# Weight blocks of the first FFN stage read from the weights themselves, and the sums of weights spread over other places

## The chip, the cores and the metric

The kernel runs on one core of a Trainium2 chip. The metric is the device time of one execution in microseconds; lower is better. Times given for a kernel are a median of several executions, and one further execution is profiled.

Engine names follow the profile: PE is TensorE (matrix products), DVE is VectorE, ACT is ScalarE, POOL is GpSimd, SP is SyncE, which issues transfers and does no arithmetic. Transfers issued by SP go through one DMA queue (q1 in the profile), those issued by POOL through another (q0). [...]

## The reference

The input x is 2 x 2048 rows of 1024 numbers, in float32. A pre-norm attention layer with one head of 256 is followed by a pre-norm feed-forward layer (FFN), cut here to what is computed:

```python
x = x + attn(layernorm(x))            # qkv = x @ Wqkv + bqkv; softmax(q k^T / 16) v; @ Wo + bo
h = layernorm(x)
logits = h @ gate_w                   # 8 experts; the two largest logits are added
r = relu(h @ up_w) ** 2               # up_w 1024 x 2048
shared = r @ down_w                   # down_w 2048 x 1024
latent = (h @ fc1_w) @ expert_w       # fc1_w 1024 x 512, expert_w 512 x 512
routed = (latent * top2_sum) @ fc2_w  # fc2_w 512 x 1024
x = x + layernorm(shared + routed) * ln_gamma + ln_beta
```

## The kernel before

**Arithmetic.** Every float32 factor is split into a rounded part and the rest, and a product is three matmuls: high x high, low x high, high x low (class `Pass3`). A "cast" on ACT makes the high part, a subtraction on DVE the low one.

**Stages.** The rows form 8 blocks of 512 (`NBLK`). First `begin` folds expert_w into fc2_w (kept in DRAM as `fc2e`) and prepares the first block; then q, k and v are made block by block (`a_block`, `qkv_block`), then attention runs over the blocks. In attention's loop `n` counts from 1 to 8: the scores of block n are made beside the value products of block n - 1, then `finish(n - 1)` and `project(n - 1)` apply Wo. `project` loads four residual rows on SP, adds bo to them by four accumulating transfers on POOL (L638, the last one kept in `last[0]`), and stores the finished rows on SP. Attention is ordered by a scheduler; `begin`, the q/k/v blocks before the last, and the FFN are in the order written.

**FFN as a seven-product scheme.** The FFN takes two blocks of rows at a time (`b` = 0 to 3) and has two stages: s = 0 multiplies by up_w and fc1_w side by side, s = 1 by down_w and fc2e one above the other. Each stage treats its weight as 2 x 2 quarters and does seven block products p1 to p7 (Strassen's scheme in Winograd's form). Three of them take a quarter of the weight as it is: p1 takes (0,0), p2 takes (1,0), p3 takes (1,1). Four take sums of quarters, numbered 1 to 4 (`RIGHT`, L777). Each product's weight comes in NK = 10 pieces of 128 x 512, so a stage has 70 pieces of 12 or more matmuls; `m` counts the pieces of the first stage.

**Sums of weights.** `sum_tile(s, q)` are DRAM tiles (`wt`), of 2 MB and 0.5 MB for each s and q. `sum_step(i)` (L387) copies one quarter into such a tile with two POOL transfers (L391); this serves for sums' first terms and also for the three plain quarters of each s. For some i it also adds the second term of an earlier sum with two accumulating transfers (L399). There are 14 steps: three in the q/k/v blocks i = 4, 5, 6 (L703) and 11 in attention, at k = 2 and k = 8 of the loops n = 2 to 7 (L746), each placed after the last bo addition issued.

**Pieces.** `stage` (L797) takes a tile `w` (pools `wk` with six and `wv` with one) and loads a piece on SP into its second half; `cast_piece` writes the high part into the first half on ACT; `end_piece` subtracts on DVE and, for pieces that are used again by a later b, stores the pair with one 512 KB POOL transfer (`w_p`, L844). Later uses load the pair and need no split. `next_piece` keeps up to three pieces ready, one cast and two loading. `wk`, `wv`, `spp` and `gp` lie in memory that attention's pools `ex` for keys and values gave back: `wk` in that of the keys, the others in that of the values. `spp` (four tiles) holds split left factors in the second stage and nothing in the first.

**Order around the start of the FFN.** The first pieces of b = 0 are loaded, cast and subtracted while attention still runs: the scheduler places them among the last scores. In b = 0 of the first stage, p1's first four pieces come first, then p1 and p2 alternate (`up_order(4)`), until m = 19; p4 follows at m = 20 to 29, p6 at 30 to 39, p5 at 40 to 49, p3 at 50 to 59 and p7 at 60 to 69. Beside them the object `norm2` normalises the second block's rows: each `step` (L942) loads a row on SP, takes moments on ACT, normalises, transposes on DVE, and writes and fetches the transposed row on POOL, in different steps for different rows, 11 steps in all. At L1156 they are spread over m = 0 to 13; from m = 12 on (`m4`, L1161) the fetched tiles are split for p4.

Of the kernel before, what the change touches and what calls it, by code (L numbers as in the profile page):

```python
# [9 lines left out]
FP = mybir.dt.float32  # L10
FR = mybir.dt.float32r
AF = mybir.ActivationFunctionType
ALU = mybir.AluOpType
# [4 lines left out]
P = 128  # L18
SQ = 32
W = 512  # L20
# [5 lines left out]
def kernel(  # L26
# [69 lines left out]
    def f32(t):  # L96
        return t.bitcast(FP)
# [223 lines left out]
    def transpose_tile(r, t, xT):  # L321

        for g in range(NCC // 4):
            pt = bank(psc, "pt")
            for j in range(4):
                nc.tensor.transpose(pt[:, ts(j, P)], r[:, ts(4 * g + j, P)], ident)
            hi, lo = (v.rearrange("p (c n) -> p c n", n=W)[:, :, ts(t, P)] for v in xT[g])
            split(pt.rearrange("p (c n) -> p c n", n=P), hi, lo)
# [30 lines left out]
    def as_piece(t, s):  # L359

        return t.rearrange("p (c n) -> p c n", n=P) if s == 0 else t

    def quarter(s, a, b):

        if s == 0:
            return [w[ts(a, HC), ts(b, n)] for w, n in ((up_w, HU), (fc1_w, HL))]
        return [w[ts(a, n), ts(b, HC)] for w, n in ((down_w, HU), (fc2e, HL))]

    def sum_tile(s, q):

        if (s, q) not in tsum:
            shapes = [(HC, n) if s == 0 else (n, HC) for n in (HU, HL)]
            tsum[s, q] = [
                dram.tile(list(sh), FP, name="wt_{}_{}_{}".format(len(tsum), s, i))
                for i, sh in enumerate(shapes)
            ]
        return tsum[s, q]

    FIRST = {1: (0, 1), 2: (1, 1), 3: (0, 1), 4: (1, 0)}
    SUMS = [(s, q) for s in range(2) for q in (1, 3, 2, 4)]
    COPIES = SUMS + [(s, q) for s in range(2) for q in ((0, 0), (1, 0), (1, 1))]
    ADDS = dict(zip((4, 5, 6, 8, 9, 10, 11, 13), SUMS))
    last = [None]

    def sum_step(i):  # L387

        s, q = COPIES[i]
        for o, t in zip(sum_tile(s, q), quarter(s, *FIRST.get(q, q))):  # L390
            nc.gpsimd.dma_start(out=o, in_=t)  # L391
        if i in ADDS:
            s, q = ADDS[i]
            if q % 2:
                terms = quarter(s, *((0, 0) if q == 1 else (1, 1)))
            else:
                terms = sum_tile(s, q // 2)
            for o, t in zip(sum_tile(s, q), terms):
                nc.gpsimd.dma_start(out=o, in_=t, accum_op=ALU.add, max_dma_last_dim=4096)  # L399


    kv = {}
# [55 lines left out]
    def begin(wqkv, xT):  # L458

        ew, f2_0 = (unit(a, FP) for a in ("ew", "f2_0"))  # L460
        ev = ew.rearrange("p (c n) -> p c n", n=LAT)
        for i in range(NLC):
            nc.sync.dma_start(out=ev[:, :, ts(i, P)], in_=cols(expert_w, i, P))
        for i in range(NLC):
            nc.sync.dma_start(out=f2_0[:, ts(i, W)], in_=fc2_w[ts(i, P), 0:W])
        f2 = [f2_0]
        first = load_block(xf, order[0])
        f2.append(load("f2_1", cols(fc2_w, 1, W))[1])

        ws = {i: load(f"w{i}", cols(Wqkv, i, D)) for i in (2, 0)}  # L470
        rows = load_block(xf, order[1])
        ws[1] = load("w1", cols(Wqkv, 1, D))
        nc.gpsimd.dma_start(out=bqk_sb, in_=bqkv[0 : 2 * D].rearrange("(f p) -> p f", p=P))
        nc.gpsimd.dma_start(out=bv_sb, in_=bqkv[2 * D : 3 * D].partition_broadcast(P))

        eh, el = unit("eh"), unit("el")
        for mc in range(NLC):
            pt = bank(psc, "pt")
            for lc in range(NLC):
                nc.tensor.transpose(pt[:, ts(lc, P)], ew[:, ds(lc * LAT + mc * P, P)], ident)  # L480
            split(pt, eh[:, ts(mc, LAT)], el[:, ts(mc, LAT)])

        def split_f2(h, eng):
            f2h, f2l = unit(f"f2h{h}"), unit(f"f2l{h}")
            for mc in range(NLC):
                split(f2[h][:, ts(mc, W)], f2h[:, ts(mc, W)], f2l[:, ts(mc, W)], eng)
            return f2h, f2l

        def fold(f2hl, first=None):
            accs = [Pass3(bank(psa, "pf"), NLC) for _ in range(NLC)]  # L490
            for mc in range(NLC):
                if first:
                    first(mc)
                for lc in range(NLC):
                    accs[lc].add(
                        piece((eh, el), mc, LAT, ts(lc, P)), piece(f2hl, mc, W, slice(0, W))
                    )
            return accs

        def folded(h, accs):  # L500
            r = unit(f"fold{h}", FP)
            for lc in range(NLC):
                nc.scalar.copy(r[:, ts(lc, W)], accs[lc].ps)
            return r

        accs = fold(split_f2(0, nc.vector))
        stats = [row_stats(first[0])]
        for t in range(NB):
            if t + 1 < NB:
                stats.append(row_stats(first[t + 1]))  # L510
            normalise(first[t], stats[t])
            if t == 0:
                f2hl = split_f2(1, nc.gpsimd)
            elif t == 2:
                wqkv[2] = split_unit(*ws[2], nc.gpsimd)
        r = [folded(0, accs)]
        r.append(folded(1, fold(f2hl, lambda t: transpose_tile(first[t], t, xT))))
        wqkv[0] = split_unit(*ws[0])
        wqkv[1] = split_unit(*ws[1], nc.gpsimd)
        return NormBlock(rows), r  # L520
# [169 lines left out]

    wqkv, xT = {}, new_xT("a")
    with tc.manual_schedule():
        norm, fold = begin(wqkv, xT)
        x3 = lambda: None
        steps = list(range(len(COPIES)))
        for i in range(NBLK - 1):
            norm, xT, x3 = a_block(i, norm, xT, x3)
            if i == 0:
                for h in range(C // W):
                    nc.gpsimd.dma_start(  # L700
                        out=cols(fc2e, h, W), in_=fold[h].rearrange("p (c n) -> p c n", n=W)
                    )
            if i >= NBLK // 2:  # L703
                sum_step(steps.pop(0))
    a_block(NBLK - 1, None, xT, x3)

    wo_f = [load_row(Wo[ts(dc, P), :]) for dc in range(NDC)]
# [75 lines left out]
            order += ([("p1", i + lag)] if i + lag < NK else []) + [("p2", i)]  # L783
        return order + [(p, i) for p in ("p4", "p6", "p5", "p3", "p7") for i in range(NK)]

    UPS = [up_order(4 if b == 0 else 1) for b in range(NBLK // 2)]
    DOWN = [(p, i) for p in ("p1", "p2", "p6", "p5", "p3", "p7", "p4") for i in range(NK)]
    NBB = NBLK // 2
    pieces = [(b, s, *w) for b in range(NBB) for s in range(2) for w in (UPS[b], DOWN)[s]]
    kept, staged, cast, ready = {}, [], [], []  # L790
    LATE = 5

    def source(s, q, i):
        t, j = (tsum[s, q][0], i) if i < HU // P else (tsum[s, q][1], i - HU // P)
        return t[:, ts(j, P)].rearrange("(c p) i -> p c i", p=P) if s == 0 else t[ts(j, P), :]

    def stage():  # L797


        b, s, p, i = pieces.pop(0)  # L800
        if len(pieces) < LATE and early:
            staged.append((early.pop(0), False, None))
            return
        n_w[0] += 1
        w = (wk if n_w[0] % 7 else wv).tile([P, 2 * W], FR, tag="w", name="w")
        if (s, p, i) in kept:
            nc.sync.dma_start(out=w.bitcast(FP), in_=kept[s, p, i])
            staged.append((w, False, None))
            return
        nc.sync.dma_start(out=as_piece(f32(w)[:, W : 2 * W], s), in_=source(s, RIGHT[p], i))  # L810

        if s == 1 and p in ("p3", "p7", "p4"):
            keep = b == 2 and p == "p4" and i >= NK - LATE
        else:
            keep = b == 1 or i % 2 == 0
        staged.append((w, True, (s, p, i) if keep else None))

    early, n_w = [], [0]  # L820

# [7 lines left out]
    def cast_piece():  # L829

        w, raw, key = staged.pop(0)
        if raw:
            nc.scalar.copy(w[:, 0:W], f32(w)[:, W : 2 * W])  # L833
        cast.append((w, raw, key))

    def end_piece():

        w, raw, key = cast.pop(0)
        if raw:
            v = f32(w)  # L840
            nc.vector.tensor_tensor(w[:, W : 2 * W], v[:, W : 2 * W], v[:, 0:W], ALU.subtract)  # L841
        if key:
            kept[key] = dram.tile([P, 2 * W], FP, name="w_{}_{}_{}".format(*key))
            nc.gpsimd.dma_start(out=kept[key], in_=w.bitcast(FP))  # L844
        ready.append((w[:, 0:W], w[:, W : 2 * W]))
# [187 lines left out]
    with tc.manual_schedule():  # L1033
        for b in range(NBB):
# [72 lines left out]
            for m, (p, i) in enumerate(UPS[b]):  # L1107
# [45 lines left out]

                if m % 2 and m < 17:
                    out_step()
                if b == 0 and m in (0, 1, 2, 4, 6, 8, 9, 10, 11, 12, 13):  # L1156
                    norm2.step()
                if b == 0 and m < NB:
                    split_x(x_t[0], 1, m, X["p2"], split_late)

                m4 = 12 if b == 0 else 10  # L1161
                if m == m4:
                    x_t[1] = norm2.x
                    X["p4"] = new_x()
# [172 lines left out]
```

## Time and profile before

| what | value |
|---|---|
| median of 3 runs (lowest to highest) | 2360.73 us (2359.38 to 2362.85) |
| the profiled execution's own time | 2357.94 us |
| its span, first to last instruction | 2355.8 us |
| PE busy / DVE / ACT / POOL | 2323.3 / 1501.8 / 1168.1 / 285.4 us |
| mean granted PE clock | 0.997 |
| moved by DMA, mean rate | 572.54 MB, 243 GB/s |
| w<-wt: piece loads from sums and copies (SP) | 280 of 256 KB |
| w_p<-w: pieces kept (POOL) | 115 of 512 KB |
| wt<-up_w and wt<-down_w (POOL), copies and additions | 9 + 9 of 2 MB |
| wt<-fc1_w and wt<-fc2e (POOL) | 9 + 9 of 0.5 MB |
| wt<-wt: second terms that are sums themselves (POOL) | 4 of 2 MB, 4 of 0.5 MB |

How to read it: the span is a little shorter than the execution's time, because work around the program's instructions is not in it. Where one engine is busy for nearly all of the span, time is found in the few stretches in which it waits, and the wait's releaser tells which transfer or engine ended it. In the lists of waits, a line gives who waited for whom, the total in us, how often, and the longest. In a timeline, the columns are start, duration, engine, line, operation, output and inputs, and in brackets the idle time before it and what ended that.

The stages in the profiled execution: q/k/v to about 310 us, attention to about 775 us with the FFN's first products mixed in from 752 us, then four rounds of the FFN.

### The profile page before, as it was taken

How to read it: one execution, taken by the hardware profiler on the slowest of the kernel's cores; microseconds unless marked ns; L12 is line 12 of the kernel's file. 1: busy time of each engine (PE TensorE's matmuls, PEld its weight loads, DVE VectorE, ACT ScalarE, POOL GpSimd, SP SyncE). 2: the span in 40 equal slices, each digit the busy share in tenths (PEclk: the TensorE clock that was granted, in tenths of full speed). 3: DMA queues.
4: the chain of work that ended last, by engine and by line, in shares of the span. 5: the costliest groups of instructions: out<-in, count | busy, mean ns of one | idle time of the engine just before them, and what ended most of it. 6: DMA issues, size and time to landing. Idle time of an engine off the chain costs nothing.

```text
span 2355.8 us, 29360 instructions
## 1 busy us (share of the span) xinstructions
PE 2323.3 (99%) x10704; PEld 1919.4 (81%) x10704; DVE 1501.8 (64%) x2238; ACT 1168.1 (50%) x1916; POOL 285.4 (12%) x425
## 2 busy tenths in 40 slices
PE   8999999999999999999999999999999999999997
PEld 7888888888887778788788888878888877888886
DVE  5566559888877575797645577753456683435656
ACT  6555455555544643667552374743055564214245
POOL 3232111011110110111110011110000021000001
PEclk9999999999999999999999999999999999999999
DMA  5977884999997766786897789786567589665674
GB/s 197 318 256 276 286 205 127 296 315 323 286 253 211 250 208 191 228 276 209 265 316 242 229 297 319 229 267 227 193 204 278 194 267 331 189 191 187 204 247 134
DMA packets 222208, 572.54 MB, mean 243 GB/s; under 512 B 18368, under 2 KB 80320, under 8 KB 220016
## 3 DMA queue, kind: packets, MB, share of 16 engines
q1 hardware_dynamic: 152160, 315.67, 39.9%
q0 software_dynamic: 69904, 255.00, 36.1%
q8 instruction: 85, 1.39, 0.2%
q14 instruction: 59, 0.48, 0.1%
HBM read 430.61 MB, written 197.66 MB: 267 GB/s over the span
## 4 chain that ended last, share of the span: by engine, by line
PE 91%; DMA 3%; issue 3%; DVE 1%; ACT 1%; POOL 0%; SPq 0%; POOLq 0%; DVEq 0%; ACTq 0%
PE pu L130 31%; PE pd L130 28%; PE po L130 7%; PE pq L130 7%; PE ps L130 7%; PE pv L130 4%; PE pw L130 4%; DMA w<-wt 2%; PE pg L890 1%; PE pf L130 1%; PE psum L622 1%; DMA xt<-xt_d 0%; DVE w L841 0%; DMA ew<-in_L_ffn_expert_w_dram 0%; DMA res<-x 0%
## 5 line engine op out<-in xcount | busy, mean ns | idle before, releaser
L130 PE MATMUL pd<-w,sp 128*128 128x512 f32 x3336 | 759.0, 389 | 4.9 <-DVE y L1274 4.8
L130 PEld LDWEIGHTS pd<-w,sp 128*128 128x128 f32 x3336 | 625.5, 188 | 137.3 <-ACT nm L260 6.0
L130 PE MATMUL pu<-xh,w 128*128 128x512 f32 x2240 | 692.8, 390 | 0.1
L130 PEld LDWEIGHTS pu<-xh,w 128*128 128x128 f32 x2240 | 419.2, 188 | 89.9 <-DVE w L841 1.5
L130 PE MATMUL pu<-xl,w 128*128 128x512 f32 x1120 | 436.2, 389 | 0.9 <-DVE xl L150 0.9
L841 DVE TENSOR_TENSOR w<-w 128x512 fp32r<-128x512 f32 x280 | 191.6, 687 | 99.0 <-ACT w L833 92.0
L833 ACT CAST w<-w 128x512 fp32r<-128x512 f32 x280 | 170.9, 615 | 166.2 <-DMA w<-wt 155.6
L130 PEld LDWEIGHTS pu<-xl,w 128*128 128x128 f32 x1120 | 210.2, 188 | 45.1 <-DVE xl L150 1.4
L1077 ACT CAST sp<-h 128x512 fp32r<-128x512 f32 x238 | 146.3, 618 | 151.9 <-PE pd L130 125.6
L1082 DVE TENSOR_TENSOR sp<-h,sp 128x512 fp32r<-128x512 f32 x238 | 162.9, 687 | 68.1 <-ACT sp L1077 67.9
L130 PE MATMUL po<-p,v 128*128 128x512 f32 x768 | 194.3, 391 | 0.6 <-DVE p L143 0.6
L130 PE MATMUL ps<-q,k 128*128 128x512 f32 x768 | 192.5, 390 | 1.5 <-DVE max L565 1.5
L130 PEld LDWEIGHTS ps<-q,k 128*128 128x128 f32 x768 | 143.6, 188 | 31.8 <-DVE max L565 1.9
L130 PEld LDWEIGHTS po<-p,v 128*128 128x128 f32 x768 | 143.0, 188 | 30.2 <-DVE p L143 1.0
L150 DVE TENSOR_TENSOR xl<-xt,xh 128x512 fp32r<-128x512 f32 x108 | 74.4, 689 | 134.9 <-ACT xh L149 134.9
L1027 ACT ACTIVATE h<-h 128x1024 f32<-128x1024 f32 x48 | 50.7, 1055 | 208.8 <-DVE h L1137 159.8
L560 ACT COPY s<-ps 128x512 f32<-128x512 f32 x128 | 75.0, 587 | 133.5 <-PE ps L130 133.4
L213 DVE STREAM_TRANSPOSE xblk<-xrow 128x1024 f32<-128x1024 f32 x60 | 121.1, 2018 | 9.6 <-ACT xrow L283 9.6
L844 POOL DMA_DIRECT2D w_p<-w x115 | 61.6, 536 | 508.7 <-DVE w L841 435.0
L565 DVE TENSOR_TENSOR max<-ps,max 128x512 f32<-128x512 f32 x120 | 82.4, 687 | 36.3 <-ACT s L560 36.1
L130 PE MATMUL pq<-xha,w_h 128*128 128x512 f32 x256 | 99.7, 389 | 0.0
L130 PE MATMUL pq<-xha,w_l 128*128 128x512 f32 x256 | 99.7, 389 | 0.0
(181 smaller groups left out, 3031.8 us busy)
## 6 DMA issues: line engine op xcount, KB each, us to landing
w<-w_p SPq DMA_DIRECT2D x280, 512.0 KB, 4.2
w<-wt SPq DMA_DIRECT2D x280, 256.0 KB, 3.4
w_p<-w POOLq DMA_DIRECT2D x115, 512.0 KB, 4.6
xt_d<-xblk POOLq DMA_DIRECT2D x56, 512.0 KB, 4.4
xt<-xt_d POOLq DMA_DIRECT2D x56, 512.0 KB, 6.7
wt<-in_L_ffn_up_w_dram POOLq DMA_DIRECT2D x9, 2048.0 KB, 23.8
wt<-in_L_ffn_down_w_dram POOLq DMA_DIRECT2D x9, 2048.0 KB, 31.1
xres<-in_L_attn_x_dram SPq DMA_DIRECT2D x32, 512.0 KB, 11.2
```

What stands on the lines that cost most here:

```text
L130: nc.tensor.matmul(self.ps, lhsT=a, rhs=b, start=self.i == 0, stop=self.i == self.n - 1, skip_group_check=self.on,)
L150: late_ops.append(lambda: nc.vector.tensor_tensor(lo, t, f32(hi), ALU.subtract))
L213: nc.vector.transpose(b.rearrange("p (q k i) -> p q k i", q=P // SQ, i=SQ), r.rearrange("p (k i q) -> p q k i", k=NCC, i=SQ),)
L560: nc.scalar.copy(s["s"][k // 4][:, ts(k % 4, W)], pm)
L565: nc.vector.tensor_tensor(s["max"], pm, s["max"], ALU.max)
L622: nc.tensor.matmul(pt[:, t : t + 1], lhsT=s["sum"][:, ds(i * W + t * P, P)], rhs=ones, start=i == 0, stop=i == 1,)
L833: nc.scalar.copy(w[:, 0:W], f32(w)[:, W : 2 * W])
L841: nc.vector.tensor_tensor(w[:, W : 2 * W], v[:, W : 2 * W], v[:, 0:W], ALU.subtract)
L844: nc.gpsimd.dma_start(out=kept[key], in_=w.bitcast(FP))
L1027: nc.scalar.activation(o, v, AF.Relu)
L1077: nc.scalar.copy(t[:, 0:W], v)
L1082: add(t[:, W : 2 * W], v, f32(t)[:, 0:W], ALU.subtract)
```

## The change

1. The q/k/v blocks hold no sum step any more. Two steps stand in `begin`, beside the transposes of the first block; 14 stand in attention, in n = 2 to 8; one is at m = 46 of the first stage of b = 0.
2. A step is one term: either the first term of a sum (two copies) or the second (two accumulating transfers). There are 8 first terms, 8 second terms and one step that copies 512 x 512 of up_w (1 MB) into a new DRAM tile `lead`: 17 steps.
3. The first stage's three plain quarters are no longer copied. Its pieces of p1, p2 and p3 are loaded from up_w and fc1_w themselves, except p1's first four pieces, which come from `lead`. A direct piece is loaded into a tile of `spp` (`raw`), not into `w`; the cast and the subtraction read `raw` and write both halves of `w`.
4. The second stage's three plain quarters are still copied, now by `copy_step` at m = 16, 26 and 36 of the first stage of b = 0.
5. The 11 steps of `norm2` stand at m = 0, 1, 2, 3, 4, 6, 7, 8, 9, 10, 11, and `m4` is 10 for every b.

In the built program the two terms of the sums reach POOL's queue thus: n = 2 gets a first term and `lead`; n = 3 to 7 each get one first and one second term; n = 8 gets the second terms of the second stage's sums 3 and 2, behind project(6)'s bo additions and ahead of project(7)'s.

```diff
-    COPIES = SUMS + [(s, q) for s in range(2) for q in ((0, 0), (1, 0), (1, 1))]
-    ADDS = dict(zip((4, 5, 6, 8, 9, 10, 11, 13), SUMS))
+    SECOND = {1: (0, 0), 2: 1, 3: (1, 1), 4: 2}
+    LEAD = 4
+    STEPS = [(a, 0) for a in SUMS[:3]]
+    for a, c in zip(SUMS, SUMS[3:] + [None] * 3):
+        STEPS += ([(c, 0)] if c else []) + [(a, 1)]
+    STEPS.insert(3, None)
+    lead = dram.tile([HC, LEAD * P], FP, name="wt_lead")
...
     def sum_step(i):
-        s, q = COPIES[i]
-        for o, t in zip(sum_tile(s, q), quarter(s, *FIRST.get(q, q))):
+        if STEPS[i] is None:
+            nc.gpsimd.dma_start(out=lead, in_=up_w[0:HC, 0 : LEAD * P])
+            return
+        (s, q), second = STEPS[i]
+        a = (SECOND if second else FIRST)[q]
+        terms = quarter(s, *a) if isinstance(a, tuple) else sum_tile(s, a)
+        for o, t in zip(sum_tile(s, q), terms):
+            if second:
+                nc.gpsimd.dma_start(out=o, in_=t, accum_op=ALU.add, max_dma_last_dim=4096)
+            else:
+                nc.gpsimd.dma_start(out=o, in_=t)
+
+    def copy_step(q):
+        for o, t in zip(sum_tile(1, q), quarter(1, *q)):
             nc.gpsimd.dma_start(out=o, in_=t)
...
-        r.append(folded(1, fold(f2hl, lambda t: transpose_tile(first[t], t, xT))))
+        def beside(t):
+            transpose_tile(first[t], t, xT)
+            if t < 2:
+                sum_step(steps.pop(0))
+
+        r.append(folded(1, fold(f2hl, beside)))
...
-            if i >= NBLK // 2:
-                sum_step(steps.pop(0))
...
+    def direct(s, p, i):
+        return s == 0 and p in ("p1", "p2", "p3") and (p, i // LEAD) != ("p1", 0)
+
+    def source(s, p, i):
+        q = RIGHT[p]
+        if s == 0 and isinstance(q, tuple):
+            parts = quarter(s, *q) if direct(s, p, i) else [lead]
+        else:
+            parts = tsum[s, q]
...
-        nc.sync.dma_start(out=as_piece(f32(w)[:, W : 2 * W], s), in_=source(s, RIGHT[p], i))
+        if direct(s, p, i):
+            raw = spp.tile([P, 2 * W], FP, tag="sp", name="raw")[:, 0:W]
+        else:
+            raw = f32(w)[:, W : 2 * W]
+        nc.sync.dma_start(out=as_piece(raw, s), in_=source(s, p, i))
...
-            nc.scalar.copy(w[:, 0:W], f32(w)[:, W : 2 * W])
+        if raw is not None:
+            nc.scalar.copy(w[:, 0:W], raw)
...
-            nc.vector.tensor_tensor(w[:, W : 2 * W], v[:, W : 2 * W], v[:, 0:W], ALU.subtract)
+            nc.vector.tensor_tensor(w[:, W : 2 * W], raw, f32(w)[:, 0:W], ALU.subtract)
...
-                if b == 0 and m in (0, 1, 2, 4, 6, 8, 9, 10, 11, 12, 13):
+                if b == 0 and m in (0, 1, 2, 3, 4, 6, 7, 8, 9, 10, 11):
                     norm2.step()
...
-                m4 = 12 if b == 0 else 10
+                if b == 0 and m in (16, 26, 36):
+                    copy_step(((0, 0), (1, 0), (1, 1))[m // 10 - 1])
+                elif b == 0 and m == 46:
+                    sum_step(steps.pop(0))
+                m4 = 10
```

## The prediction

> **What bounds the kernel now.** I read the engine rows first, then TensorE's waits, then the timelines around those waits.
>
> ```profile
> PE 2323.3 (99%) x10704; PEld 1919.4 (81%) x10704; DVE 1501.8 (64%) x2238; ACT 1168.1 (50%) x1916; POOL 285.4 (12%) x425
> ```
> ```profile
> PE pt L480 <- DMA ew<-in_L_ffn_expert_w_dram: 7.2, 2, 3.7
> PE pd L130 <- DVE y L1274: 4.8, 3, 2.0
> PE pv L130 <- ACT xha L142: 2.2, 1, 2.2
> PE ps L130 <- DVE max L565: 1.5, 1, 1.5
> ...
> PE pu L130 <- DVE xl L150: 0.9, 1, 0.9
> ```
>
> TensorE is busy 2323.3 of 2355.8 us and no matmul is added or removed. So the change can win only from these waits and can lose only by making new ones. The waits it comes near are 2.2 us (end of q/k/v), 1.5 us (end of attention) and 0.9 us (first block of the first stage): 4.6 us in all. The start (7.2) and the three waits for y (4.8) it does not touch.
>
> The 1.5 us wait matters most. In the timelines of SyncE, ScalarE and TensorE:
>
> ```profile
> 705.64 5.46 SPq L810 DMA_DIRECT2D w<-wt  x5
> ```
> ```profile
> 705.64 0.59 ACT L560 COPY s<-ps 128x512 f32<-128x512 f32 x1 [2.13 <-PE ps L130]
> 711.90 0.62 ACT L833 CAST w<-w 128x512 fp32r<-128x512 f32 x1 [5.66 <-DMA w<-wt]
> 712.42 0.58 ACT L560 COPY s<-ps 128x512 f32<-128x512 f32 x1
> ```
> ```profile
> 710.88 1.52 PE L130 MATMUL po<-p,v 128*128 128x512 f32 x6
> 713.89 1.66 PE L130 MATMUL ps<-q,k 128*128 128x512 f32 x6 [1.49 <-DVE max L565]
> ```
>
> The first FFN piece is cast on ScalarE in the middle of the last scores. ScalarE works in order, so until that 256 KB load lands (711.87) no score bank is copied out, and TensorE runs dry. Every further microsecond of this load is one of TensorE. The load is issued when TensorE has finished with the keys whose memory it takes over (705.45), not earlier. In the built program TensorE's order is unchanged, and ScalarE's and VectorE's are too up to the first directly read piece, so this cast stays where it is.
>
> **The change part by part.** Landings and packets below are single records of the trace. A plain pair of copies (2 MB + 0.5 MB) occupies POOL's ring 8 us: the one issued at 237.69 landed 254.50, the transfer before it 246.50. An accumulating pair takes 12.5 us from an input (595.75 to 608.29, SyncE's queue silent) and about 13.1 us from another sum (it moves 0.40 MB in 2 us, 444 to 448). That is about 39 records of 4 KB on each DMA engine at 0.335 us. POOL's ring works in order.
>
> *Start:* two copy pairs enter POOL's queue at about 31.2 (end of its split at 26.59 + 4.62). Four issues at 0.65 us fit in POOL's idle 12.5 us before 43.74; 2 x 8 us of ring end near 48, and the next transfer of the ring is issued at 52.35. Nothing. If they ran 8 us over, the first x tile (landed 62.3) would come near 66, while the next block needs it at 72.7: still nothing.
>
> *Three copies leave q/k/v.* The one wait there (278.28, 2.2 us) follows a fetch that stands ahead of the last copy in the ring:
>
> ```profile
> 270.54 0.77 POOL L224 DMA_DIRECT2D xt<-xt_d  x1 [5.40 <-issue]
> 271.30 0.56 POOL L450 DMA_DIRECT2D q_d<-q  x1
> 271.85 0.66 POOL L391 DMA_DIRECT2D wt<-in_L_ffn_up_w_dram  x1
> ```
>
> The earlier copy had landed at 254.50. What makes the fetch late is SyncE's q and Wo loads (261.72 to 270.52), which stay. Gain 0.
>
> *Attention to n = 7:* 11 copies and 8 adds become 6 copies, the 1 MB lead and 5 adds. TensorE has one 0.6 us gap there, on a softmax split. Gain 0, but the ring now empties each round: with n = 6's pairs done by about 611 and n = 7's by about 660, it is idle when SyncE starts project(6)'s transfers at 672.
>
> *n = 8 gets two adds* (the second terms of the second stage's sums 3 and 2); before, nothing stood there. They follow the fourth bo add of project(6). Before, that one was issued at 704.91, because its residual row, asked for at 681.12, landed only at 704.36 beside an add. With an idle ring I work out 686 for that landing (two rows and three stores of 1.3 us each beside bo adds of 2.5 us), the bo add ending at 690.5, the first add 12.5 us later at 703, the second at 716.1. The load of the first piece sends its first packets at 708.6. How do the two queues share an engine? Between 709 and 710 the bo add (4 KB records) has 36 records and the piece's load (512 B records) has 35: one for one, whatever their size. So of the load's 512 records, 32 on an engine, 22 each wait for an add record (7.5 us / 0.335): 22 x 0.362 = 8.0 us, the other 10 x 0.027 = 0.3, landing 0.5 after: **717.4 instead of 711.87, +5.5 us**, all of it on TensorE. The other three lead pieces follow 0.9 us apart and are not late. Ends: if the adds are done before 708.6 the load lands near 709 and the 1.5 us wait goes (-1.5); if all 32 pair, 708.6 + 11.6 + 0.5 = 720.7 (+8.8).
>
> A rule speaks otherwise: the Trainium skill, "DMA: Bandwidth & Descriptors", section on queues, rings and completion order, says an engine changes queue only at packet ends, a packet being some 9 to 17 descriptors. The load would need at most four turns, each behind one 4 KB record: 4 x 0.335 = 1.3 us, landing 708.6 + 0.85 + 1.3 + 0.5 = 711.3, a term of -0.6. The row shows one for one in a microsecond in which each engine handled about two of each, so I take +5.5.
>
> *x rows of p1* (SyncE 730 to 740) would meet the adds only if those ran past 730.
>
> *Lead and direct pieces:* the same bytes in the same 512 B records; cast (0.615) and subtraction (0.687) are the same forms. In a direct piece SyncE no longer waits for the w tile, ScalarE's cast does; queued behind it are PSUM evictions, with five other banks free. A w tile is free about six pieces of 2.73 us before its reuse and cast three before: no wait. The raw tile returns only after VectorE's subtraction, so SyncE asks about five pieces ahead instead of six; a load takes 3 to 4 us. Nothing.
>
> *Second rows earlier:* before, p4's first matmul waits (0.93) for the last xl:
>
> ```profile
> 831.88 0.69 DVE L1123 TENSOR_TENSOR h<-pu,rwb 128x512 f32<-128x512 f32 x1 [0.71 <-PE pu L130]
> 832.49 0.68 DVE L150 TENSOR_TENSOR xl<-xt,xh 128x512 fp32r<-128x512 f32 x1
> ```
>
> Its fetch was issued at 822.52. Row loads move past one SyncE piece load and the writes and fetches past one or two kept stores; all come two pieces (5.5 us) sooner. ScalarE's 15.5 us for four rows now fall in six pieces instead of seven, a lag of up to 4 us against three pieces of lead. **-0.9 us.**
>
> *Copies at m = 16, 26, 36:* 40 records beside loads: 40 x (0.17 + 0.027) = 7.9 us; a piece load beside it lands after 8.3 instead of 3 us, the next kept store 8.5 after issue instead of 4.3. Piece loads have some 10 us to spare (issued 851.32, landed 854.12, used 867.7, after cast and subtraction). 0; if the copy took twice as long, 2 us each.
>
> *The add at m = 46:* 40 records at 0.335 let only 40 of the loads' records an engine through in 15 us, 1.25 loads where 5.4 are wanted. But four raw tiles are free, so p3's first four pieces are in by then; the fifth lands about 53.6 pieces after the start, where it must be multiplied at 54 after 1.3 us of cast and subtraction: 0 to 4 us, **+0.7** taken.
>
> *b = 1's direct pieces* take a sp buffer three pieces before the stage ends, when a w tile would come free too: 0.
>
> Sum: +5.5 - 0.9 + 0.7 = **+5.3 us**. Against the profiled execution's 2357.94 that is 2363.2; the median of the runs, 2360.73, lies 2.8 above that execution, and with it the forecast is **2366.0**.
>
> **Rivals.**
> - *The adds drain in time* (ends on the other side). If project(6)'s last bo add ends before 683, both adds are over at 708.6 and the first load lands alone: -1.5 - 0.9 = 2358.3. For it: the ring really is idle from 660. Against it: the row is asked for at 681.12, behind a store of project(6) that TensorE's pace sets. 13%.
> - *The load is not held up one for one* (the rule's case): -0.6 - 0.9 + 0.7, 2360. 10%.
> - *The m = 46 add starves the pieces:* beside the forecast +4 to +10, about 2373. For it: 1.25 loads in 15 us. Against: the four free raw tiles. 10%.
> - *The backlog stays:* the bo add again at 705, both adds 711 to 740, first piece at 722.5, the fourth near 742: +28 less 0.9, 2388. For it: that is when it was issued before. Against: 5 copies and an add less before it. 7%.
> - The forecast itself: 60%, own range 2363 to 2370.
>
> **Numbers.** Less than 0.2% (4.7 us) can't be told from no change. The forecast's term of +5.5 is good to about 3 us, so some 60% of it lies over 2365.5; with the two worse rivals slower gets 0.55, the rest of the forecast and most of the first two rivals 0.40, faster 0.05, since the waits within reach hold 4.6 us. The range is 2358.5 (first rival) to 2376 (third).
>
> **What would show it.** The wait of ps for max at 712 grows from 1.5 to about 7 us, with ScalarE idle for w<-wt; the first-piece load takes about 12 us instead of 6.2; two wt<-wt or wt<-down_w adds are issued near 687; the 0.93 wait for xl is gone; the 2.2 at 278 stays; at most 1 us of new wait at p3. It is wrong if the first load lands by 712, or if a wait of several us stands in stage one's pieces.

## The result and the profile after

| | before | after |
|---|---|---|
| median, runs taken side by side (lowest to highest) | 2362.00 us (2359.38 to 2362.94) | 2379.86 us (2377.94 to 2384.75) |
| the profiled execution's own time / its span | 2357.94 / 2355.8 us | 2380.22 / 2378.5 us |
| mean granted PE clock | 0.997 | 0.993 |

The ratio is 1.0082, with a 95% interval of 1.0068 to 1.0096: the changed kernel is slower by 16 to 23 us. 2366.0 was forecast, in a range that ended at 2376. The direction was right and the size was not.

The row of engines on the page of the changed kernel:

```profile
PE 2329.8 (98%) x10704; PEld 1923.3 (81%) x10704; DVE 1501.5 (63%) x2238; ACT 1168.4 (49%) x1916; POOL 282.2 (12%) x420
```

TensorE has the same 10704 matmuls. It is busy 6.5 us longer although its work is the same, so some matmuls ran slower; the rest of the 22.7 us of span is waiting. The list of TensorE's waits (who waited for whom, total us, times, longest):

```profile
PE ps L130 <- DVE max L582: 12.2, 2, 9.8
PE pt L491 <- DMA ew<-in_L_ffn_expert_w_dram: 6.1, 3, 3.8
PE pu L130 <- DVE w L868: 5.7, 3, 3.4
PE pd L130 <- DVE y L1305: 3.1, 2, 1.7
PE pv L130 <- ACT xha L142: 2.8, 1, 2.8
PE pu L130 <- ACT w L861: 1.6, 1, 1.6
...
PE pu L130 <- ACT xh L149: 0.7, 1, 0.7
```

Against the list of before, the wait for max at attention's end grew from 1.5 to 12.2 us, two rows of waits for pieces of the first stage (w, on DVE and on ACT) are new with 7.3 us together, a wait for xh of 0.7 is new, and the 0.9 for xl is gone. The wait at the end of q/k/v (pv for xha) stayed, at 2.8.

Since both kernels run the same matmuls in the same order, each matmul's start can be set against its twin's. The shift of the later one, worked out from the two traces:

```
stretch of the changed kernel            what stands there                        TensorE's shift, us
start to 280                             (run to run)                              -0.4
attention's end, 712 to 730              wait for max, half clock, wait for max   +13.1  (8.1 + 2.0 + 3.0)
first stage, 800 to 824                  wait for xh, 0.72, and for w, 0.29        +1.9
first stage, 841 to 846                  first direct pieces, half clock           +3.4  (1.85 + 1.55)
first stage, 850                         wait for xl gone                          -0.9
first stage, p3, 944 to 953              waits for w, half clock                   +6.8  (1.6 + 3.65 + 1.55)
later                                    (run to run)                              -0.7
sum                                                                               +23.2
```

The table compares two single executions, whose times differ by 22.3 us; the medians differ by 17.9, since the profiled execution of the kernel before (2357.94) lies below all five of its timed ones.

Attention's end first. What POOL issues there, by its timeline (start, duration, engine, line, operation, output and inputs; in brackets the idle time before and what ended it):

```profile
692.53 0.86 POOL L655 DMA_DIRECT2D xres<-in_L_attn_bo_dram  x1 [11.17 <-DMA xres<-in_L_attn_x_dram]
693.06 1.64 POOL L404 DMA_DIRECT2D wt<-in_L_ffn_down_w_dram  x1
...
694.41 3.09 POOL L404 DMA_DIRECT2D wt<-wt  x2
```

These are the two adds of n = 8 (each an accumulating transfer, which adds to what stands in its destination, in two parts), behind the last bo addition, which waited for its residual row until 692. By single records of the trace the bo addition landed at 697.5, the two parts of the first add at 709.8 and 712.8, and those of the second at 723.8 and 726.6. SyncE issues the loads of the four lead pieces meanwhile:

```profile
705.07 10.34 SPq L838 DMA_DIRECT2D w<-wt_lead  x4
```

They landed at 719.6, with seven microseconds of the second add still to come, and at 726.8, 727.6 and 728.3, as it ended. ScalarE's timeline:

```profile
705.07 0.59 ACT L577 COPY s<-ps 128x512 f32<-128x512 f32 x1 [2.13 <-PE ps L130]
719.62 0.62 ACT L861 CAST w<-w 128x512 fp32r<-128x512 f32 x1 [13.95 <-DMA w<-wt_lead]
...
726.86 1.36 ACT L861 CAST w<-w 128x512 fp32r<-128x512 f32 x2 [5.20 <-DMA w<-wt_lead]
```

It stands at the first cast for 13.95 us and at the second for 5.20 us, and copies no bank of scores meanwhile. TensorE's timeline answers:

```profile
710.32 1.52 PE L130 MATMUL po<-p,v 128*128 128x512 f32 x6
721.61 2.93 PE L130 MATMUL ps<-q,k 128*128 128x512 f32 x6 [9.78 <-DVE max L582]
724.34 2.76 PE L130 MATMUL po<-p,v 128*128 128x512 f32 x6
729.49 1.65 PE L130 MATMUL ps<-q,k 128*128 128x512 f32 x6 [2.39 <-DVE max L582]
```

Two things are to be read. The stall is 9.78 us and a second one of 2.39 us follows. And between them six matmuls take 2.93 and 2.76 us where they took 1.52: the clock is halved, as the row of that stretch in the table by windows has it (us, then busy time and instructions of each engine, granted clock, DMA share, GB/s):

```profile
714.00:728.00 14.00, 5.49 (x12) 3.81 (x12) 3.01 (x4) 3.06 (x5) 0.00 (x0) 0.51 1.02 219
```

At p3, ScalarE's and TensorE's timelines:

```profile
945.29 0.62 ACT L861 CAST w<-raw 128x512 fp32r<-128x512 f32 x1 [17.12 <-DMA raw<-in_L_ffn_up_w_dram]
```
```profile
945.96 0.50 PE L130 MATMUL pu<-xh,w 128*128 128x512 f32 x1 [1.56 <-ACT w L861]
949.84 0.79 PE L130 MATMUL pu<-xh,w 128*128 128x512 f32 x1 [3.38 <-DVE w L868]
```

The fifth direct piece of p3 is cast 17 us after the fourth: its load was asked for at 930.08 and landed at 945.19, beside the add of m = 46 (issued 925.62, landed 940.82 and 944.45). Both gaps come from this one piece. The first is for its high part, the cast. The second is for its low part: on VectorE the subtraction stands behind xl, a low part of x, whose high part xh ScalarE cast only at 947.86, behind the late piece and two steps on finished results (945.82 and 946.90). VectorE's timeline:

```profile
948.50 0.69 DVE L150 TENSOR_TENSOR xl<-xt,xh 128x512 fp32r<-128x512 f32 x1 [8.81 <-ACT xh L149]
949.10 0.68 DVE L868 TENSOR_TENSOR w<-raw,w 128x512 fp32r<-128x512 f32 x1
```

### The profile page after: what moved, and what is told of

The parts are those of the page before. It is cut to its first block, busy times and chain, and to the rows that moved or that the text cites. A ratio compares the mean times of both kernels' runs of the same rounds, so it can differ in the third digit from the quotient of the medians.

```text
span 2378.5 us, 29270 instructions
## 1 busy us (share of the span) xinstructions
PE 2329.8 (98%) x10704; PEld 1923.3 (81%) x10704; DVE 1501.5 (63%) x2238; ACT 1168.4 (49%) x1916; POOL 282.2 (12%) x420
## 4 chain that ended last, share of the span: by engine, by line
PE 88%; DMA 5%; issue 2%; ACT 2%; DVE 2%; POOL 0%; SPq 0%; POOLq 0%; DVEq 0%; ACTq 0%
PE pu L130 30%; PE pd L130 28%; PE po L130 7%; PE ps L130 7%; PE pq L130 6%; PE pw L130 4%; PE pv L130 3%; DMA w<-wt 1%; PE pg L917 1%; PE pf L130 1%; DMA w<-wt_lead 1%; DMA raw<-in_L_ffn_up_w_dram 1%; DMA xt<-xt_d 1%; PE psum L639 1%; DVE xblk L213 0%
## 5 line engine op out<-in xcount | busy, mean ns | idle before, releaser
L861 ACT CAST w<-w 128x512 fp32r<-128x512 f32 x241 | 147.0, 615 | 157.5 <-DMA w<-wt 115.3
L868 DVE TENSOR_TENSOR w<-w 128x512 fp32r<-128x512 f32 x241 | 164.9, 686 | 85.9 <-ACT w L861 80.8
L130 PE MATMUL ps<-q,k 128*128 128x512 f32 x768 | 193.9, 392 | 12.2 <-DVE max L582 12.2
```

The source lines that it names most:

```text
L130: nc.tensor.matmul(self.ps, lhsT=a, rhs=b, start=self.i == 0, stop=self.i == self.n - 1, skip_group_check=self.on,)
L861: nc.scalar.copy(w[:, 0:W], raw)
L868: nc.vector.tensor_tensor(w[:, W : 2 * W], raw, f32(w)[:, 0:W], ALU.subtract)
```

## The experiments

Eleven variants follow, in four groups; a ratio is to the kernel before as it ran beside the same group (2361.64, 2359.71, 2360.29 and 2360.09 us). A difference in us between kernels of different groups is good to about 2 us. The expectations speak of theories by letters; they are, in short: A, the records of a piece's load wait one for one behind those of an add, and the in-order engine that casts the piece holds TensorE up; the others are rivals to it or to each other.

### Where the loss comes from

**No add at n = 8 nor at m = 46.** The three adds are spread elsewhere: three steps go back into q/k/v.

```diff
+            if i >= NBLK // 2:
+                sum_step(steps.pop(0))
...
-                elif b == 0 and m == 46:
-                    sum_step(steps.pop(0))
```

> The changed kernel with three sum steps back in the q/k/v blocks i = 4 to 6, so that attention's n = 8 and m = 46 hold none. Theory A (piece loads share the DMA engines record for record with the accumulating transfers): the waits at the end of attention (13.1 us lost there, the halved clock in it) and at p3 (6.8 us) both go, 2379.9 - 19.9 = 2360; the wait of ps for max falls from 12.2 to 1.5 us or less and the first piece's load takes under 7 us instead of 14.5. Rival B (the loss comes from reading up_w itself or from the earlier second rows): the time stays over 2375. Rival C (sums in q/k/v cost there what they save later): the wait of pv at 278 us grows by several us.

Measured: 2361.70 us, ratio to before 0.9998 (0.9989 to 1.0006). There is no wait for max, the first lead load took 2.9 us (705.73 to 708.62), and nothing stands at p3. The wait at the end of q/k/v is 2.1. So the whole loss, in sum, hangs on the three adds' places, and steps in q/k/v cost nothing. The small gaps of the second rows and the direct reads stay (0.72, 0.29 and 1.34 us); the waits for max (1.5) and xl (0.9) that are gone make up for them. Rivals B and C fell.

**The changed kernel without the add at m = 46.**

```diff
-                elif b == 0 and m == 46:
-                    sum_step(steps.pop(0))
```

> The changed kernel without the step at m = 46; it leaves out the second term of the second stage's sum 4. Theory A: the wait at p3 (1.6 + 3.7 us, and 1.6 us of halved clock after it) goes, 2379.9 - 6.8 = 2373. Rival D (the wait at p3 comes from direct loads having only four raw tiles): it stays, 2380.

Measured: 2375.43 us, 1.0063 (1.0048 to 1.0078). The gaps at p3 are gone and the wait for max stayed, 10.9 us; rival D, that the four raw tiles are short even without the add, fell. The time fell by 4.4 us, less than the 6.8 read from the traces. The adds of n = 8 alone are worth 2375.43 - 2361.70 = 13.7 us.

**The add at m = 46 alone.** Two steps in q/k/v, none at n = 8.

```diff
+            if i >= NBLK - 3:
+                sum_step(steps.pop(0))
...
-            if k in (2, 8) and n > 1 and steps:
+            if k in (2, 8) and 1 < n < NBLK and steps:
```

> The changed kernel with its transfers moved so that the last attention block (n = 8) issues none (two steps go back into q/k/v, n = 2 to 7 hold two each) while the add at m = 46 stays. Theory A (the m = 46 add starves p3's direct pieces by itself: four raw tiles are the whole look-ahead, and the add shares the queues for some 18 us): no wait for max at attention's end as in the kernel with all adds in q/k/v (2361.7), but the two gaps at p3 (about 1.6 and 3.4 us) and the half clock after them stay, 2361.7 + 5 to 7 = 2367 to 2369. Rival I (p3 is late only because n = 8's adds and the halved clock delayed everything before it): no gaps at p3, 2361 to 2363.

Measured: 2366.76 us, 1.0026 (1.0017 to 1.0034). The two gaps at p3 are what they were, 1.52 and 3.38 us, with no stall at attention's end before them. In the view of the tile raw between 898 and 935, the list of who waited for it:

```profile
  ACT w L863: 18.8, 2
...
  PE pu L130: 4.9, 2
```

So this add costs some 6.5 us by itself (2366.76 against 2360.23 of the next kernel, which lacks it), and the rival that made it a follower of n = 8's delay fell.

**One add at n = 8, none at m = 46.**

```diff
+            if i >= NBLK - 3:
+                sum_step(steps.pop(0))
...
-                elif b == 0 and m == 46:
-                    sum_step(steps.pop(0))
```

> Half the dose: no add at m = 46, and n = 8 issues one add (sum 4's second term, sum to sum) in place of two; two steps are back in q/k/v. Theory A (every record of the lead's first load waits for one record of an add while adds are in the ring): the one add follows the last bo add (issued about 692.5) and ends about 706 to 713, the load is issued at about 705.5, so it pairs for 0 to 7 us and lands between 709 and 714; the wait for max is 0 to 3 us, no long half clock, time 2362 to 2366. Rival J (anything at n = 8 that makes project(6) late stalls attention's end, whatever its length): wait for max 8 us or more, 2370 to 2376.

Measured: 2360.23 us, 1.0002 (0.9993 to 1.0010). The add's two parts, issued at 690.0 and 690.6, landed at 704.9 and 707.4. ScalarE's timeline:

```profile
704.13 0.59 ACT L577 COPY s<-ps 128x512 f32<-128x512 f32 x1 [2.13 <-PE ps L130]
708.30 0.62 ACT L863 CAST w<-w 128x512 fp32r<-128x512 f32 x1 [3.58 <-DMA w<-wt_lead]
```

The first lead load took 4.15 us, the cast waited 3.58, and there is no wait for max at all. One add costs nothing and two cost 13.7 us: the loss is a backlog that must be gone when SyncE asks for the first pieces, not a price per add.

### How the adds at n = 8 stop TensorE

**The lead tile stored piece by piece**, so that a load is 128 records of 2 KB instead of 512 of 512 bytes. Everything else is the changed kernel.

```diff
-    lead = dram.tile([HC, LEAD * P], FP, name="wt_lead")
+    lead = dram.tile([LEAD * P, HC], FP, name="wt_lead")
...
+            for j in range(LEAD):
+                nc.gpsimd.dma_start(
+                    out=lead[ts(j, P), :].rearrange("p (c n) -> p c n", n=P),
+                    in_=up_w[0:HC, ts(j, P)].rearrange("(c p) n -> p c n", p=P),
+                )
```

> The changed kernel with the lead tile laid out so that a lead piece is read in 128 records of 2 KB instead of 512 of 512 bytes; the same bytes, the adds unmoved. Theory A: 8 records an engine instead of 32 wait for an add record (0.33 to 0.36 us), so the first piece lands about 713 instead of 719.6 and all four by 722 instead of 728; the wait of ps falls from 12.2 to some 4 us, the half-clock stretch shortens, time 2369 to 2372. Rival E (the queues share by bytes, or the load is late for another reason): first piece still near 719, 2380.

Measured: 2376.40 us, 1.0066 (1.0051 to 1.0081). The loads landed at 714.2, 717.7, 721.2 and 724.5 instead of 719.6 to 728.3, and ScalarE's first wait was halved:

```profile
714.21 0.62 ACT L867 CAST w<-w 128x512 fp32r<-128x512 f32 x1 [7.17 <-DMA w<-wt_lead]
```

Counting records started in 2 us while both queues were full, on all 16 engines together:

```
                                POOL's ring : SyncE's queue, per 2 us
changed kernel, 512 B loads     91:95  93:91  95:94  93:93          (adds' records 4 KB)
this kernel, 2 KB loads         86:81  80:85  80:79  84:83  81:79
```

Equal counts alone would also fit turns of several records on either side. The spacing does not: in the changed kernel each of nine successive stretches of 0.345 us from 713.0 on holds 16 starts of each queue, as many as there are engines. So the queues take turns record by record, whatever a record holds. With a quarter of the records the first load took 7.7 us instead of 14.5, and the others followed some 3.5 us apart. In both, about 3.6 us pass before the load's first record starts (1.05 in the kernel without the adds); the records take the other 4.2 and 10.9. Sharing by bytes, the rival, fell. The wait for max was 5.3 us in two stalls, near the 4 expected, but the time, 2376.40, missed the 2369 to 2372 expected; it fell by only some 3.5 us from 2379.86: each of the four pieces now held ScalarE for a while, and two stretches of half clock remained.

**The first four casts on GpSimd.** The loads stay late; the casts leave ScalarE. The add at m = 46 is left out, so that the 2375.43 above is its base.

```diff
-            nc.scalar.copy(w[:, 0:W], raw)
+            if n_cast[0] < LEAD:
+                nc.gpsimd.tensor_copy(w[:, 0:W], raw)
+            else:
+                nc.scalar.copy(w[:, 0:W], raw)
+            n_cast[0] += 1
```

> The changed kernel without the add at m = 46 (as in the run without it, the second term of the second stage's sum 4 is left out: 2375.4 there), with the first four casts of pieces on GpSimd in place of ScalarE. The loads stay as late as they are (about 719 to 728). Theory A (TensorE stalls because ScalarE, in order, stands at the first cast and copies no score bank): the wait for max and the long half clock go, 2375.4 less 12 to 13 = 2362 to 2364, unless GpSimd, now standing there itself, issues the last block's bo adds late (then up to 3 more, as a wait of pw's rows). Rival N (attention's end is slowed by the transfers themselves, through rows of q, x or of project(6)): the wait for max stays at 8 us or more, 2372 to 2376.

Measured: 2361.56 us, 1.0004 (0.9995 to 1.0012). SyncE's row for the loads, and TensorE's timeline in the stretch that held the stall:

```profile
704.59 10.78 SPq L838 DMA_DIRECT2D w<-wt_lead  x4
```
```profile
712.56 1.52 PE L130 MATMUL po<-p,v 128*128 128x512 f32 x6
713.92 1.52 PE L130 MATMUL ps<-q,k 128*128 128x512 f32 x6
```

The loads landed at 719.5, 725.5, 726.2 and 727.0, as late as ever, and TensorE passes 712 to 730 without a gap and at full clock. The time returned in full. So it is not the transfers that slow attention's end: it is one cast that waits for a transfer ahead of ScalarE's score copies. GpSimd did not stand at the loads in ScalarE's place; its timeline:

```profile
744.56 0.89 POOL L655 DMA_DIRECT2D xres<-in_L_attn_bo_dram  x1 [48.29 <-DMA xres<-in_L_attn_x_dram]
...
751.86 0.63 POOL L862 CAST w<-w 128x512 fp32r<-128x512 f32 x1
```

The casts come behind the bo additions of project(7), whose first waited for its residual row, and so long after the loads had landed. The edit thus moved the casts in time as well as to another engine; TensorE's order differs only from 749 on, behind the stretch of the stall.

### The FFN's start: direct reads and the second rows

**The norm's list and `m4` of the change alone, in the kernel before.**

```diff
-                if b == 0 and m in (0, 1, 2, 4, 6, 8, 9, 10, 11, 12, 13):
+                if b == 0 and m in (0, 1, 2, 3, 4, 6, 7, 8, 9, 10, 11):
...
-                m4 = 12 if b == 0 else 10
+                m4 = 10
```

> The kernel before with only the second rows' steps moved up and the split for p4 from m = 10. As predicted: the 0.9 us wait for xl at p4's start goes and nothing else changes, 2361. Rival F (the steps packed into m = 0 to 11 overload ScalarE and VectorE and make the new waits that the changed kernel shows at 800 to 845 us): waits of pu of 2 to 4 us there, 2364 to 2366.

Measured: 2359.61 us, 0.9992 (0.9983 to 1.0001). The 0.93 for xl is gone, but two gaps are new, 0.72 at 785.5 (for xh) and 0.24 at 809.0 (for w): nothing is won. (A gap of 1.34 at 1213.7, in the next round, is not explained.) ScalarE's and TensorE's timelines at the first:

```profile
784.25 1.04 ACT L259 ACTIVATE junk<-xrow 128x1024 bf16<-128x1024 f32 x1
...
785.53 0.60 ACT L149 CAST xh<-xt 128x512 fp32r<-128x512 f32 x1
```
```profile
786.18 0.73 PE L130 MATMUL pu<-xh,w 128*128 128x512 f32 x2 [0.72 <-ACT xh L149]
```

The step that moved to m = 3 puts a row's moments on ScalarE ahead of the last cast of p2's x.

**The direct reads alone**: the kernel without adds at n = 8 and m = 46, with the norm's list and `m4` of before (the diff above, turned round).

> The kernel with all adds in q/k/v and none at m = 46, with the norm of the second rows where it was in the kernel before (steps at m = 0, 1, 2, 4, 6, 8 to 13; x of p4 at m = 12): the direct reads alone. Theory K (the gap near 826 is the norm's xt traffic moved onto the first direct pieces' loads): the gap near 826 goes, the 0.93 us wait for xl near 832 comes back, the small gaps near 785 and 809 go; 2360.5 to 2362. Rival L (the direct pieces make it without the norm's help): a gap of 1 us or more at the first direct pieces stays beside the 0.93, 2362 to 2363.5.

Measured: 2361.84 us, 1.0011 (1.0003 to 1.0019). TensorE's timeline:

```profile
827.65 0.50 PE L130 MATMUL pu<-xh,w 128*128 128x512 f32 x1 [2.37 <-DVE w L870]
...
834.55 0.50 PE L130 MATMUL pu<-xl,w 128*128 128x512 f32 x1 [0.93 <-DVE xl L150]
```

The 0.93 is back, the two small gaps are gone, and at the end of the first direct pieces stands a gap of 2.37 us, larger than the 1.34 with the moved norm. The direct reads make it themselves: their last two loads there, asked for at 814.0 and 815.2, took 9.5 and 8.9 us beside x fetches of 512 KB and kept stores on POOL's ring.

**Twice as many raws.** Two direct pieces share one tile of `spp`; base is the kernel without adds at n = 8 and m = 46 (2361.70).

```diff
-            raw = spp.tile([P, 2 * W], FP, tag="sp", name="raw")[:, 0:W]
+            if not halves:
+                t = spp.tile([P, 2 * W], FP, tag="sp", name="raw")
+                halves.extend((t[:, 0:W], t[:, W : 2 * W]))
+            raw = halves.pop(0)
```

> The kernel with all adds in q/k/v and none at m = 46 (2361.7), with two direct raw pieces to one tile of the pool sp, so that twice as many raws can be asked for ahead. Theory G (the wait of 1.3 us at the FFN's start, about 826, comes from raw tiles that return late, so that SyncE asks late): that wait goes or shrinks under 0.5, 2359.5 to 2361. Rival H (the loads there are slow because POOL's ring of x fetches and kept stores shares the DMA engines with them; look-ahead isn't the limit): the wait stays within 0.5 us of 1.3, 2361 to 2362.5.

Measured: 2358.98 us, 0.9998 (0.9990 to 1.0007). The gap near 826 is gone (0.2 us of wait for w in the whole run). The last two direct loads of p1 and p2 were asked for at 805.3 and 805.7 instead of 814.3 and 814.9, and landed by 812.9 instead of 824.3. So the look-ahead was the limit, although the loads it lacked were slow because of shared queues. In time nothing can be told: both kernels stand at 0.9998 of the kernel before.

**The same two raws to a tile, with the add at m = 46.**

> The kernel with the add at m = 46 alone (two gaps at p3 of 1.5 and 3.4 us, 2366.8), with two direct raw pieces to one tile of the pool sp. Theory A (the four raw tiles are the limit: the fifth raw is asked for only as the add is under way): now eight raws are asked for by about 904 us and land before or just after the add starts, the ninth lands at about 928 and is needed about 938; both gaps go, 2359.5 to 2361.5. Rival M (the add shares the queues for 18 us, in which too few pieces come in whatever the look-ahead): a gap of 2 us or more stays at p3, 2363 to 2367.

Measured: 2358.93 us, 0.9995 (0.9985 to 1.0005), against 1.0026 with single raws. Eight raws were asked for from 898.7 to 905.6 and were in by 911.0; the add was issued at 907.4 and landed at 922.7 and 925.4; the ninth raw, asked for at 914.0, took 13.1 us to 927.1, and nobody waited. Both gaps at p3 are gone.

### The whole change with both mended

The changed kernel with all its transfers where they are, the first four casts on GpSimd and two raws to a tile.

> The whole changed kernel (two adds at n = 8, the add at m = 46, no transfer in q/k/v) with two edits: the first four casts of pieces on GpSimd, and two direct raws to one tile of sp. Theory A with G (its loss is the two blocked casts and the raws' look-ahead, and no part of it is the transfers as such): no wait for max, no gap at 826 or at p3, less the 0.93 us for xl: span 2353 to 2356, time 2357 to 2360 against 2360.3 to 2361.6 of the kernel before, which is within what can be told from no change. Rival O (the adds at n = 8 and the one at m = 46 together leave too little room even so): a new gap of 2 us or more at p3 or at the FFN's first pieces, 2362 to 2367.

Measured: 2359.88 us, 0.9997 (0.9989 to 1.0005). No wait for max, no gap at 826 or at p3, though the lead loads again landed as late as 722.0 to 727.6. Its profiled span, 2359.9, lies above the 2353 to 2356 expected: outside the change, the waits for y are 1.8 us longer than before and two more stretches of half clock stand at 1140 and 1928, and the two small gaps (0.72 for xh, 0.27 for w), which that sum had left out, stayed. It gives back the loss and wins nothing that can be measured; so do the others. No version here beats the kernel before.

## Why the prediction was wrong

**The mechanism of +5.5 was right and its size was not.** It was said that the first lead load pairs record for record with n = 8's adds, that ScalarE stands at its cast and that TensorE pays. All three were seen, and the runs with 2 KB records and with GpSimd's casts show the first and the other two separately. The rule weighed against the row (whole packets of 9 to 17 descriptors before an engine changes queue, section on queues, rings and completion order of the Trainium skill's "DMA: Bandwidth & Descriptors") was said to give -0.6. That took the add's turn to be a single 4 KB record, which the section doesn't say. If an add's turn were a packet too, the load would take two to four turns and wait some 11 to 12 us in them (an estimate from the section's figure and 0.335 us a record), about the upper bound of the prediction. So the counts, 93:93 and 80:79, only refuse the -0.6; it is the even spacing that refuses packets. But the term measured 13.1 us, for three reasons.

- *When the adds end.* Said: last bo addition over at 690.5, adds over at 703 and 716.1. Measured: 697.5, 712.8 and 726.6. Of the 10.5 us, 7.0 are the bo addition: its residual row landed at 692 and not at 686, since it took 11.4 us beside the third bo addition, which itself took 11.3. The prediction put each bo addition at 2.5 us of an empty ring, but rows, stores and additions share the engines both ways. And the last 2.2 us of both (689.3 to 691.5) are one DMA engine alone: it handled a 16 KB record of the queue for instructions (q8, 689.26, 0.95 us) ahead of its last two records of each, when the others had none left. 2.8 more are the first add, 15.3 us for the 12.5 taken, and 0.7 the second.
- *How much pairs.* Said: 22 of the load's 32 records on an engine. With the adds still running until 726.6, all 32 paired, and the load took 14.5 us. This was the upper bound (+8.8, landing at 720.7): the load landed at 719.6, and TensorE's first stall shifted it by 8.1.
- *What follows.* "The other three lead pieces follow 0.9 us apart and are not late" failed outright: the second piece's records paired too, it landed 7.2 us behind the first, and it gave a second stall worth 3.0. And no step priced a slower clock after a stall: 2.0.

**The +0.7 for m = 46 failed by a factor of six to ten**: 6.8 us between the traces of the changed kernel and the one before, about 6.5 for the add alone, 4.4 between the medians with and without it. "Four raw tiles are free, so p3's first four pieces are in by then" held, and so did a fifth piece that is late by 0 to 4 us: it landed at 945.19, 15.1 us after it was asked for, and TensorE, free from 944.4, waited 1.6 us for its high part. What failed is "after 1.3 us of cast and subtraction". The low part was ready at 949.78, 4.6 us after the landing, because ScalarE had stood 17 us at the cast with other work queued behind, and VectorE's subtraction stood behind that work: 3.65 us more. For the half clock, 1.55, no term was put. The rival that this add starves the pieces, at 10%, had the size (+4 to +10), and the prediction's own sign of being wrong, a wait of several us in stage one's pieces, came (3.38).

**"Nothing" for the direct pieces failed**: 3.4 us in the changed kernel (1.85 of wait, 1.55 of half clock). It was seen that raws come back a piece later and that SyncE asks later; it was taken that "a load takes 3 to 4 us", which is the row of a quiet queue. There, beside the norm's fetches and kept stores, it took 9.4.

**The -0.9 for xl came, and was given back.** The work of four rows in six pieces was said to be covered by a lag of up to 4 us against three pieces of lead. It wasn't: a shift of 1.9 us around a wait for xh and one for w in the changed kernel, and 0.96 us in the same two waits with the norm alone.

**Right:** no gain at the end of q/k/v (the wait of 2.2 stayed, 1.7 to 2.8 in all kernels, with the fetch still issued late, when the write of the row that it fetches had landed, though the weight copy behind it is gone):

```profile
269.35 0.77 POOL L224 DMA_DIRECT2D xt<-xt_d  x1 [5.24 <-DMA xt_d<-xblk]
```

Also right: the start, and nearly so the copies at m = 16, 26 and 36. They landed 10.4 to 14.7 us after issue and a load beside them took up to 14.8, where some 8 was said, so the spare 10 us were used up: most kernels show no wait there, two show one (0.88 at 888, 0.70 at 902).

The rival "the backlog stays" (7%, 2388) came nearest in kind for n = 8: it had adds over at 740 and first piece at 722.5, against 726.6 and 719.6. Its cause, a ring that never empties, was not seen: the ring was empty by 672.3 (660 was said), when project(6)'s transfers began. The truth lay between it and the forecast, and the range left it out. (The first rival's sum, 2358.3, leaves out the +0.7 of m = 46; with it, it is 2359.0.)

## What to carry to other kernels

A transfer that is hidden on its own queue is paid by whoever shares the DMA engines and by everything queued behind the instruction that waits for it: price it at the busy ring's rate, and ask which in-order engine stands at its landing. The first things to try against such a stall are to put the waiting instruction on an engine with nothing urgent behind it, or to ask earlier, with more buffers; here one of each took the whole loss away, without moving a transfer. A backlog has a point from which it costs: one add was free and two cost 13.7 us, so such a term needs its date of emptying, with an error on it, before any per-record sum.

## What the runs showed of the hardware

- **A stall is paid partly twice.** In the stall of 9.78 us (711.8 to 721.6) and behind it the granted clock was one half for 13.65 us (714.2 to 727.8), so that TensorE began again at half speed and lost 2.0 us more. Around a stall of 10.9 us it was again 13.65, and around the pair of 1.5 and 3.4 us at p3 6.83 in one run and 3.41 in another. Every such stretch inside the kernels is a multiple of 3.41 us, the window that the Trainium skill's "TensorE: Matmul & The Clock Gate" gives (Part 1, on the clock gate). The page has the clock fall after an idle window of that length; here single gaps of 2 to 3 us were enough in some runs (1.99 us, then 3.41 at half clock) and not in others (2.37 us and none near it).
- **Two queues alternate by single records** once both have records under way: 16 and 16 in each 0.345 us at 4 KB against 512 bytes, and 80:79 in 2 us at 4 KB against 2 KB. A load of 512-byte records that takes 2.9 us alone takes 14.5 us beside an add.
- **An accumulating transfer is a long neighbour**: at m = 46 the 2 MB part landed 15.2 us after issue and the 0.5 MB part behind it 18.2 us after its own, at 0.33 us for a 4 KB record (0.18 for a 2 KB one in the adds at n = 8).
